# A planned graph-attention kernel: one shared set of five edge-weight places, new durations in its planner, and the last attention but one kept for the end

## The chip, the cores and the metric

The kernel runs on one core of one Trainium2 chip. The metric is device time in microseconds; the median of three runs before the change is 3646.97 us (3645.85 to 3647.93). The core has a matrix engine (PE, TensorE), a vector engine (DVE), a scalar engine (ACT), GpSimd (POOL) and a queue engine for transfers (SP, SyncE). Each runs its own list of instructions strictly in the order in which the program wrote it, and waits on semaphores where it needs another's result.

## The reference

The input is 32 graphs of 512 nodes, with 512 float32 features per node (`x`) and a sparse 0/1 adjacency (`adj`). Two residual layers follow one another.

```python
# layer 0
h = relu(layernorm(x))
s = leaky_relu((h @ w_src)[:, :, None] + (h @ w_dst)[:, None, :] + b, 0.2)
x = x + softmax(where(adj + eye == 0, -inf, s), axis=-1) @ h
# layer 1: two graph attention layers over mask = adj > 0 or diagonal
h = relu(layernorm(x))
def gat(h, W, a_src, a_dst):            # per head
    xl = h @ W
    e = leaky_relu((xl . a_src)[:, None] + (xl . a_dst)[None, :], 0.2)
    return softmax(where(mask, e, -1e9), axis=source).T @ xl
h = elu(concat(gat(h, W1, ...) for 4 heads of 256) + b1)
x = x + gat(h, W2, ...)                 # one head of 512
         + b2
```

Per graph there are thus six matrices of 512 x 512 edge weights: one in layer 0, four for the heads of W1, one for W2.

## The kernel before

**Stages.** Per graph b the stages are: `layer0_scores` (layer norm, dot products with the two attention vectors on DVE at L384, edge weights), `layer0_out` (attention, added to x), `layer1_in` (layer norm, 16 transposes on PE, x spilled to DRAM), `layer1_project` (products with W1, by Strassen's scheme with seven products in place of eight; the sums of the quarters are `combine`, L881 on DVE or L882 on POOL), `layer1_scores` and `layer1_head` for the four heads, `layer2_project` (products with W2 and its edge weights), and `layer2_out` (attention, added to x, stored). The main loop at the end of the kernel writes them down so that stages of neighbouring graphs stand side by side: `layer2_out(b - 1)` after `layer1_project(b)`, `layer0_out(b + 1)` after the heads of b, `layer0_scores(b + 2)` before `layer2_project(b)`. All matmuls of the attentions are on L684, all of the projections on L900, transposes on L506 and L605.

**Edge weights.** `edge_weights` makes one matrix E of four tiles of 128 x 512. The row of source terms is spread over the partitions (by PE transposes, or through DRAM by two DMAs); four L643 on DVE take the masked maximum; L649 and L651 (four numbers per partition) make from it the bound m of each row; m is spread by four transposes on PE (L506) or through DRAM; then per tile ACT computes the leaky ReLU (L665), DVE subtracts m (L668), POOL adds the mask (L671) and ACT takes the exponential (L674). PE then reads E as the stationary side of `aggregate` (L684), DVE takes a reciprocal (L696 or L970) and scales and adds (L702 or L973). The heads of W1 then go through elu: for three of the four (TURNED) on ACT (L987, L990), DVE (L994), and a transposing DMA between two ACT copies (L558, L574); for the last on ACT (L1009), DVE (L1013) and eight transposes on PE.

**What sets the order.** Nothing in the main loop runs at once. Each `op(...)` notes an operation with its engine or engines, its cost, what it reads and writes, and a head start or delay in rank. A cost is a pair: how long the engine is occupied, and when the result is there (for DMAs more). `Plan.run` then makes drafts: a list schedule in which each engine takes, whenever it is free, the ready operation of lowest rank, with 60 ns for a signal between engines; each first draft is ranked anew by the latest times that follow from it. The draft that ends first by the planner's own costs is written out as the program, so the costs decide the order on each engine, but not how long anything takes on the chip. Operations with `lock=True` on DVE and POOL are kept from overlapping each other in the draft; L649 and L651 have no lock, L1013, L671 and L882 have one.

**Places.** Each buffer of the plan belongs to a kind with a fixed number of places. A buffer takes a free place with its first operation and returns it after its last. Kinds named in the tuple of `Plan(slots, (...))` give their places out strictly in the order in which the program first names the buffers; other kinds give them to whichever operation is ready. Before, "E" has three places (heads, and the sums of the projections: one place for W1, two for W2) and "E_one" two (layer 0 and W2); both are given out in turn. All these places have the same shape, [128, 4, 512] float32.

**The end.** Graph 30's last attention (`layer2_out(B - 2)`) is split: `EARLY = 1` of its four tiles stands in the last round of the loop, before the heads of graph 31, and the other three after the last `layer2_project`, followed by the attention of graph 31.

The adjacency is loaded by `load_adj` (L725, on POOL's queue, with cast); the first load has a cost of its own. L758 adds the identity to it for layer 0, L761 turns it into a mask, and a transposing DMA makes the transposed mask.

Of the kernel before, what the change touches and what calls it, by code (L numbers as in the profile page):

```python
# [16 lines left out]
P = 128  # L17
# [229 lines left out]
def on_act(n, per_partition=0):  # L247

    one = n / 1.2 + (95.0, 140.0, 280.0)[per_partition]
    return one, one + 60.0  # L250

# [17 lines left out]
def kernel(  # L269
# [24 lines left out]
    nc = tc.nc  # L294
    B, N, D = x.shape
    H, F = att_src1.shape
    HF = H * F
    T = N // P
# [22 lines left out]
    def places(kind, n, shape, dtype=F32, pool=big):  # L321
# [12 lines left out]
        "xl2": places("xl2", 1, [P, T, 2 + D + 1]),  # L334
        "E": places("E", 3, [P, T, N]),
        "E_one": places("E_one", 2, [P, T, N]),
        "v": places("v", 4, [P, 2, F]),
# [114 lines left out]

    def scores_2(att):
        part = const.tile([P, KH, 2], F32, name="part")
        for k in range(KH):
            (q, r), kk = QUARTER[k // (KH // 2)], k % (KH // 2)
            lo, hi = w2_s[q][:, kk, :], w2_s[r][:, kk, :]
            for i in range(2):
                op(
                    "DVE", on_dve(W2),  # L460
                    lambda lo=lo, i=i, k=k: dot(lo[:, 2:], flat(att[1])[:, i * D : i * D + W2 - 2], part[:, k, i : i + 1]),
                    W["w2"]((q, kk)) + att[1](i), W["w2"](("part", k)), -LATER, lock=True,
                )
                op(
                    "DVE", on_dve(W2),
                    lambda lo=lo, hi=hi, i=i: dot(hi, flat(att[1])[:, i * D + W2 - 2 : (i + 1) * D], lo[:, i : i + 1]),
# [68 lines left out]
    def evict(src, dst, src_of, dst_of, n, bias=None, psum_half=False):  # L535
# [12 lines left out]

        op(("ACT", "DVE"), (on_act(n, bias is not None), on_dve(n)), (by_act, by_dve), src, dst)

    def turned(values_of, src, place, results_of, dst):
# [4 lines left out]
        op(  # L556
            "ACT", (1040.0, 1100.0),
            lambda: nc.scalar.copy(  # L558
# [19 lines left out]

        op("ACT", (1160.0, 1220.0), pair, src, dst)

# [52 lines left out]

    def edge_weights(kind, scores, ac, lines, k, mask_max, mask, near):

# [18 lines left out]

        E = Buffer(kind)
        m_row = (
# [61 lines left out]
    def load_adj(b, m):  # L718
# [67 lines left out]
    def layer0_scores(b):  # L786
        rstd, nmr = layernorm(X[b])
        h0, ac = Buffer("h"), Buffer("ac")
        for t in range(T):
            relu_normed(h0, X[b], t, rstd, nmr)  # L790
            for i, w in ((1, ws_r), (0, wd_r)):
                op(
                    "DVE", on_dve(D), lambda t=t, w=w, i=i: dot(h0.at[:, t, :D], w, ac.at[:, i, t : t + 1]),
                    h0(t) + W["w0"](0, 1), ac((i, t)), lock=True,
# [8 lines left out]

        L0[b] = (h0, edge_weights("E_one", scores, ac, in_lines(first(ac, 2), scores, 2) if b else None, 0, m0, m0T, not b))

# [143 lines left out]
    def layer1_scores(b, h):  # L949
# [8 lines left out]
        ac, lines = AC[b]  # L958
        return edge_weights("E", ac(0), ac, lines, 2 * j, m1T, m1, True)

# [71 lines left out]
    def layer2_project(b):  # L1032
# [19 lines left out]
        )  # L1052
        L2[b] = (edge_weights("E_one", ac(0), ac, in_lines(first(ac, 2), ac(0), 2) if b < B - 1 else None, 0, m1T, m1, b == B - 1), xl)

# [18 lines left out]

    EARLY = 1
    load_x(0)
# [63 lines left out]
```

## Time and profile before

| | |
|---|---|
| runs | 3647.93, 3645.85, 3646.97 us; median 3646.97 |
| the profiled execution | 3648.51 us, of it 3646.7 from the first to the last instruction (the span) |
| granted clock of PE, mean | 0.994 |
| busy, share of the span | PE 97%, its weight loads 83%, DVE 78%, ACT 62%, POOL 39% |
| moved by DMA | 378.82 MB, 104 GB/s |

The profile is of one execution. "L684" is line 684 of the kernel; a line can be that of a helper that many stages call, so the names of the tiles (E, E_one, h, xl, pair) tell the stage. In a row of the timeline the columns are start and duration in us, engine, line, instruction, result and operands, a count, and in brackets how long the engine was idle before and what ended that. In the view of waits: who waited for whom, us in total, how often, the longest. A group's row has the busy time in us, the mean of one in ns, then the engine's idle time before it and what ended it. Each matmul of this kernel stands in the records twice (the four heads make 2048 matmuls in the code and 4096 records on L684), so 16 records are 8 matmuls. The times of matmuls include their pipelined ends; their issue is closer together.

### The profile page before, as it was taken

To read this page: it belongs to the slowest core of one execution; us is meant where nothing else is said; L and a number is where in the kernel's file an instruction comes from. 1 tells how busy PE (TensorE), PEld (TensorE's weight loads), DVE (VectorE), ACT (ScalarE), POOL (GpSimd) and SP (SyncE) were. 2 spreads that over 40 slices of the span, in tenths; PEclk is the share of its full clock that TensorE was granted. 3 is DMA by queue.
4 is the path that set the end of the run, shared out by engine and by line. 5 is a ranking of instruction groups with operands and counts; after the bars stand their busy time and mean duration, and the time that the engine had idled before them with its cause. 6 is when DMAs were issued, how large, how long until landed. Compare 5 with 4: busy or idle time off the path is not lost.

```text
span 3646.7 us, 50543 instructions
## 1 busy us (share of the span) xinstructions
PE 3542.6 (97%) x16852; PEld 3036.1 (83%) x16852; DVE 2851.2 (78%) x7367; ACT 2264.6 (62%) x3929; POOL 1424.6 (39%) x1279
## 2 busy tenths in 40 slices
PE   4899999999999999999999999999999999999998
PEld 3788888888888888888888888888888888888887
DVE  7978778877778877778787788877787877887755
ACT  2666566665666665666666667655666656666554
POOL 4534334434334343334343344343343433343422
PEclk9999999999999999999999999999999999999999
DMA  6244433444433444334443334443334443344321
GB/s 172 77 105 119 104 92 104 100 121 113 96 96 103 104 121 112 90 96 105 115 116 98 95 103 99 125 116 86 97 110 105 119 108 89 103 103 118 105 73 41
DMA packets 510374, 378.82 MB, mean 104 GB/s; under 512 B 348344, under 2 KB 386976, under 8 KB 510112
## 3 DMA queue, kind: packets, MB, share of 16 engines
q1 hardware_dynamic: 476320, 342.03, 32.8%
q0 software_dynamic: 33792, 33.56, 6.1%
q8 instruction: 132, 2.16, 0.2%
q14 instruction: 130, 1.06, 0.1%
HBM read 257.16 MB, written 68.01 MB: 89 GB/s over the span
## 4 chain that ended last, share of the span: by engine, by line
PE 80%; DVE 14%; ACT 2%; issue 1%; DMA 1%; POOL 0%; DVEq 0%; ACTq 0%; SPq 0%
PE acc L684 45%; PE acc L900 32%; DVE junk L384 5%; PE acc L506 3%; DVE v L1013 1%; DVE hT L881 1%; DVE hT L545 1%; DVE col L521 1%; DVE col L649 1%; ACT h L529 1%; DVE v L973 1%; PE acc L605 1%; DVE junk L643 1%; DVE E L881 1%; DVE xl L913 1%
## 5 line engine op out<-in xcount | busy, mean ns | idle before, releaser
L684 PE MATMUL acc<-pair,E 128*128 128x257 f32 x4096 | 920.4, 379 | 2.4 <-ACT row L987 2.4
L684 PEld LDWEIGHTS acc<-pair,E 128*128 128x128 f32 x4096 | 771.7, 189 | 115.5 <-ACT row L987 2.8
L671 POOL TENSOR_TENSOR E<-E,m 128x512 f32<-128x512 f32 x512 | 605.1, 1211 | 455.3 <-DVE E L668 396.7
L900 PE MATMUL acc<-w_T,E 128*128 128x257 f32 (+1 forms) x2048 | 517.9, 380 | 0.8 <-POOL w_T L488 0.8
L684 PE MATMUL acc<-h,E_one 128*128 128x256 f32 (+1 forms) x2048 | 491.2, 381 | 8.6 <-ACT E_one L674 7.5
L684 PE MATMUL acc<-xl,E_one 128*128 128x257 f32 x1984 | 447.9, 381 | 2.7 <-ACT E_one L674 2.7
L643 DVE CUSTOM_DVE_ANT_0 junk<-m1T,acc 128x512 bf16<-128x512 bf16 x640 | 436.6, 682 | 11.4 <-PE acc L506 3.4
L900 PEld LDWEIGHTS acc<-w_T,E 128*128 128x128 f32 x2048 | 385.4, 189 | 61.0 <-POOL w_T L488 1.5
L684 PEld LDWEIGHTS acc<-h,E_one 128*128 128x128 f32 x2048 | 380.8, 191 | 63.6 <-ACT E_one L674 8.3
L684 PEld LDWEIGHTS acc<-xl,E_one 128*128 128x128 f32 x1984 | 371.8, 190 | 54.7 <-ACT E_one L674 3.1
L674 ACT ACTIVATE E<-E 128x512 f32<-128x512 f32 x512 | 315.6, 623 | 161.7 <-POOL E L671 161.4
L913 DVE TENSOR_TENSOR pair<-acc,pair 128x258 f32<-128x258 f32 (+1 forms) x390 | 165.4, 426 | 293.7 <-PE acc L900 219.2
L539 ACT COPY pair<-acc 128x258 f32<-128x258 f32 (+1 forms) x456 | 165.8, 370 | 320.5 <-PE acc L900 315.8
L665 ACT ACTIVATE E<-row,ac 128x512 f32<-128x512 f32 x512 | 341.1, 707 | 2.4 <-DMA row<-lines 2.4
L668 DVE TENSOR_TENSOR E<-E,acc 128x512 f32<-128x512 f32 x512 | 330.4, 678 | 6.5 <-PE acc L506 3.1
L671 POOL TENSOR_TENSOR E_one<-E_one,m0T 128x512 f32<-128x512 f32 x128 | 144.4, 1152 | 355.6 <-DVE E_one L668 355.6
L725 POOL DMA_DIRECT2D m<-in_adj_dram x64 | 51.5, 805 | 590.8 <-DVE col L643 540.7
L900 PE MATMUL acc<-w,hT 128*128 128x258 f32 x1024 | 265.5, 384 | 0.6 <-issue 0.5
L900 PE MATMUL acc<-w,E 128*128 128x257 f32 (+1 forms) x1024 | 264.2, 380 | 0.0
L702 DVE SCALAR_TENSOR_TENSOR x<-acc,r,x 128x256 f32<-128x256 f32 x512 | 239.7, 479 | 30.9 <-PE acc L684 22.8
L529 ACT ACTIVATE h<-x,col,col 128x512 f32<-128x512 f32 x256 | 187.6, 804 | 109.0 <-DVE col L521 109.0
L539 ACT COPY xl<-acc 128x257 f32<-128x257 f32 x218 | 77.6, 369 | 284.9 <-PE acc L900 284.8
(113 smaller groups left out, 6171.9 us busy)
## 6 DMA issues: line engine op xcount, KB each, us to landing
row<-lines SPq DMA_DIRECT2D x442, 256.0 KB, 3.4
x<-in_x_dram SPq DMA_DIRECT2D x32, 1024.0 KB
m<-in_adj_dram POOLq DMA_DIRECT2D x64, 512.0 KB, 6.3
spill<-x SPq DMA_DIRECT2D x32, 1024.0 KB, 4.2
x<-spill SPq DMA_DIRECT2D x32, 1024.0 KB
out_dram<-x SPq DMA_DIRECT2D x30, 1024.0 KB, 4.2
v<-row SPq DMA_TRANSPOSE x192, 2.7
out_dram<-x SPq DMA_DIRECT2D x8, 256.0 KB, 2.0
```

Source lines behind the costliest of these rows:

```text
L384: nc.vector.scalar_tensor_tensor(junk[:, : vector.shape[1]], values, 1.0, vector, op0=ALU.mult, op1=ALU.mult, accum_out=out)
L529: lambda: nc.scalar.activation(h.at[:, t, :D], X.at[:, t, :], AF.Relu, bias=nmr.at[:, t : t + 1], scale=rstd.at[:, t : t + 1]),
L539: nc.scalar.copy(dst_of(), src_of())
L643: lambda t=t: nc.vector.tensor_tensor_reduce(by_blocks(junk), mask_row(mask_max, t), by_blocks(a_row.at), 1.0, LOWEST, ALU.add, ALU.max, a ...
L665: lambda t=t: nc.scalar.activation(E.at[:, t, :], c_row.at, AF.Prelu, bias=a_of(t), scale=1.0, alpha=SLOPE),
L668: op("DVE", on_dve(N), lambda t=t: nc.vector.tensor_sub(E.at[:, t, :], E.at[:, t, :], m_row.at), m_row(*ROW) + E(t), E(t))
L671: lambda t=t: nc.gpsimd.tensor_add(by_blocks(E.at[:, t, :]), by_blocks(E.at[:, t, :]), mask_row(mask, t)),
L674: op("ACT", on_act(N), lambda t=t: nc.scalar.activation(E.at[:, t, :], E.at[:, t, :], AF.Exp), E(t), E(t))
L684: lambda s=s: nc.tensor.matmul(acc.at[:, :n], E.at[:, s, node_block(t)], of(s), start=(s == 0), stop=(s == T - 1)),
L702: lambda acc=acc, r=r, f=f, t=t: nc.vector.scalar_tensor_tensor(X.at[:, t, f], acc.at[:, :HD], r.at, X.at[:, t, f], op0=ALU.mult, op1=ALU. ...
L900: lambda k=k: nc.tensor.matmul(acc.at[:, :width], at[a]()[:, k, node_block(r)], weight_of(w, k, c), start=(first and k == 0), stop=(k == n ...
L913: op("DVE", on_dve(width), lambda: nc.vector.tensor_add(place(), acc.at[:, :width], place()), acc(0) + token, token)
```

## The change

The change alters no instruction and no size. It has four parts.

- "E" and "E_one" become one kind "E" with five places. It is taken out of the tuple of kinds given out in turn, so any operation that is ready can take a free place. `edge_weights` loses its parameter `kind`.
- ACT's costs in the planner: operations with one per-partition operand get 46 ns more of occupation (186 for 140), every result is there 130 ns after that (60 before); copies out of PSUM get a formula of their own (`on_act_copied`); the two copies around the transposing DMA become 945 for 1040 and 1062 for 1160.
- DVE's costs: the dot products with attention vectors are told as if 125 elements longer (130 ns), the masked maxima L643 as N + 10 for N + 60 elements. The first adjacency load is told to land after 11000 ns, not 5500.
- `EARLY = 0`: all four tiles of graph 30's last attention stand after the last `layer2_project`.

```diff
 def on_act(n, per_partition=0):
 
-    one = n / 1.2 + (95.0, 140.0, 280.0)[per_partition]
-    return one, one + 60.0
+    one = n / 1.2 + (95.0, 186.0, 280.0)[per_partition]
+    return one, one + 130.0
+
+
+def on_act_copied(n):
+    one = n / 1.2 + 52.0
+    return one, one + 160.0
...
-        "E": places("E", 3, [P, T, N]),
-        "E_one": places("E_one", 2, [P, T, N]),
+        "E": places("E", 5, [P, T, N]),
...
-    plan = Plan(slots, ("x", "spill", "m0", "m0T", "m1", "m1T", "h", "hT", "pair", "xl2", "E", "E_one", "v"))
+    plan = Plan(slots, ("x", "spill", "m0", "m0T", "m1", "m1T", "h", "hT", "pair", "xl2", "v"))
...
-                        "DVE", on_dve(F),
+                        "DVE", on_dve(F + 125),
...
-                    "DVE", on_dve(W2),
+                    "DVE", on_dve(W2 + 125),
...
-        op(("ACT", "DVE"), (on_act(n, bias is not None), on_dve(n)), (by_act, by_dve), src, dst)
+        op(("ACT", "DVE"), (on_act_copied(n) if bias is None else on_act(n), on_dve(n)), (by_act, by_dve), src, dst)
...
-            "ACT", (1040.0, 1100.0),
+            "ACT", (945.0, 1100.0),
...
-        op("ACT", (1160.0, 1220.0), pair, src, dst)
+        op("ACT", (1062.0, 1220.0), pair, src, dst)
...
-    def edge_weights(kind, scores, ac, lines, k, mask_max, mask, near):
+    def edge_weights(scores, ac, lines, k, mask_max, mask, near):
...
-                "DVE", on_dve(N + 60),
+                "DVE", on_dve(N + 10),
...
-        E = Buffer(kind)
+        E = Buffer("E")
...
-            "POOL", (1100.0, 5500.0) if first else (2200.0, 16000.0 if early else 8000.0), lambda: nc.gpsimd.dma_start(m.at, node_tiles(adj, b)),
+            "POOL", (1100.0, 11000.0) if first else (2200.0, 16000.0 if early else 8000.0), lambda: nc.gpsimd.dma_start(m.at, node_tiles(adj, b)),
...
-                    "DVE", on_dve(D), lambda t=t, w=w, i=i: dot(h0.at[:, t, :D], w, ac.at[:, i, t : t + 1]),
+                    "DVE", on_dve(D + 125), lambda t=t, w=w, i=i: dot(h0.at[:, t, :D], w, ac.at[:, i, t : t + 1]),
...
-    EARLY = 1
+    EARLY = 0
```

The three calls of `edge_weights` drop their first argument, and the other line of `scores_2` changes as the one shown.

More of the change, by code (lines that the diff above doesn't have):

```diff
@@ L464, in scores_2 @@
                 op(
-                    "DVE", on_dve(W2),
+                    "DVE", on_dve(W2 + 125),
                     lambda lo=lo, hi=hi, i=i: dot(hi, flat(att[1])[:, i * D + W2 - 2 : (i + 1) * D], lo[:, i : i + 1]),
@@ L802, in layer0_scores @@
         scores = c + ac(*((0, t) for t in ROW))
-        L0[b] = (h0, edge_weights("E_one", scores, ac, in_lines(first(ac, 2), scores, 2) if b else None, 0, m0, m0T, not b))
+        L0[b] = (h0, edge_weights(scores, ac, in_lines(first(ac, 2), scores, 2) if b else None, 0, m0, m0T, not b))
     def layer0_out(b):
@@ L958, in layer1_scores @@
         ac, lines = AC[b]
-        return edge_weights("E", ac(0), ac, lines, 2 * j, m1T, m1, True)
+        return edge_weights(ac(0), ac, lines, 2 * j, m1T, m1, True)
     def layer1_head(b, h, E):
@@ L1052, in layer2_project @@
         )
-        L2[b] = (edge_weights("E_one", ac(0), ac, in_lines(first(ac, 2), ac(0), 2) if b < B - 1 else None, 0, m1T, m1, b == B - 1), xl)
+        L2[b] = (edge_weights(ac(0), ac, in_lines(first(ac, 2), ac(0), 2) if b < B - 1 else None, 0, m1T, m1, b == B - 1), xl)
     def xl2_of(buf):
```

## Prediction

> **What bounds the kernel now.** I read the page first: its busy shares, its 40 slices, its chain of the work that ended last. TensorE carries the span, and the slices fall below 9 tenths for PE only at the two ends.
>
> ```profile
> PE 3542.6 (97%) x16852; PEld 3036.1 (83%) x16852; DVE 2851.2 (78%) x7367; ACT 2264.6 (62%) x3929; POOL 1424.6 (39%) x1279
> ```
>
> Busy PE time has pipelined ends in it, so I took the work from issue intervals. In the chain, 40 matmul records last 8.68 us, 0.217 us each, and 4 transposes 0.44 us, 0.110 each. The page counts 1492 transposes (520+512+256+16 on L506, 188 on L605), so 15360 of PE's 16852 are matmul records: 15360 x 0.217 + 1492 x 0.110 = 3497 us. The span is 3646.7: **150 us are all that any order of the work can win.** Next I asked for busy time by stretches. The kernel repeats every 110.81 us (the same L684 runs of 98 records stand in the chain at 2798.34 and 2909.16), from 190.4 to 3403.9 us 29 times:
>
> ```profile
> 2739.01:2849.82 110.81, 109.87 (x527) 94.42 (x526) 87.88 (x226) 70.84 (x124) 43.30 (x39) 1.00 0.39 105
> ...
> 3620.00:3647.00 27.00, 17.82 (x68) 14.54 (x68) 8.97 (x24) 4.33 (x8) 4.49 (x4) 0.77 0.10 39
> ```
>
> The columns are length, then busy us and instructions of PE, PEld, DVE, ACT and POOL, then clock and DMA. One period holds 480 records and 46 transposes: 104.2 + 5.1 = 109.2 us, so 1.6 us are lost in each, 46 us in 29. The remaining 104 us lie in the start (some 80) and the end (some 23). No other engine is full in a period (DVE 79%), so the losses are places where PE, which runs its list strictly in order, reached an instruction too early. The view of waits, PE alone, names two of them, each 30 times:
>
> ```profile
> PE acc L506 <- DVE col L651: 23.8, 30, 4.4
> ...
> PE acc L506 <- DVE v L1013: 9.8, 30, 1.9
> ```
>
> The timeline of one period gives their sizes as delay of PE's next start: 0.75 us at the transposes of m (L651), 0.40 at those of the last head's v (L1013), and 0.29 at L605, which waits for the dot products and L798 (25.6 us in 30 waits for the weight load, the first 9.7). Together **1.44 of the 1.6 us**. Why m is late:
>
> ```profile
> 2786.38 1.06 DVE L649 TENSOR_TENSOR col<-ac,col 128x4 f32<-128x4 f32 x1
> ...
> 2788.58 0.65 PE L506 MATMUL acc<-ident,col 128*128 128x128 f32 x4 [0.58 <-DVE col L651]
> ```
>
> L649 adds four numbers per partition, 0.15 us elsewhere, and here takes 1.06, while GpSimd runs four mask additions (L671) from 2782.92 to 2787.43. That is a collision of two engines, no misjudged duration. At the start, two misjudged durations show:
>
> ```profile
> 8.51 0.17 DVE L513 BATCH_NORM_AGGREGATE mv<-st 128x2 f32<-128x6 f32 x1
> 14.18 0.29 DVE L758 TENSOR_TENSOR m<-m,ident 128x128 bf16<-128x128 bf16 x1 [5.51 <-DMA m<-in_adj_dram]
> 14.39 0.17 DVE L513 BATCH_NORM_AGGREGATE mv<-st 128x2 f32<-128x6 f32 x1
> ```
>
> VectorE idles 5.51 us for the first adjacency, and the last step of the first layer norm stands behind that wait although its input came at 6 us.
>
> ```profile
> 73.17 0.38 PE L605 MATMUL acc<-ident,ac 128*8 128x128 f32 x1 [9.30 <-DVE ac L798]
> ...
> 78.66 2.01 PE L900 MATMUL acc<-w_T,E 128*128 128x258 f32 x8 [0.79 <-POOL w_T L488]
> ```
>
> Here PE stands 9.3 us behind dot products. And the end:
>
> ```profile
> 3543.56 3.79 PE L684 MATMUL acc<-xl,E_one 128*128 128x257 f32 x8 [2.70 <-ACT E_one L674]
> ...
> 3618.20 1.09 PE L506 MATMUL acc<-ident,ac 128*128 128x128 f32 x8 [0.70 <-ACT ac L539]
> 3622.29 1.11 PE L506 MATMUL acc<-ident,col 128*128 128x128 f32 x4 [3.00 <-DVE col L651]
> 3626.15 16.71 PE L684 MATMUL acc<-pair,E_one 128*128 128x257 f32 x64 [2.74 <-ACT E_one L674]
> ```
>
> From 3617.52 to 3626.15 PE does 12 transposes (1.3 us) and idles 7.3: the last weights are being made and nothing is left to run.
>
> **The change part by part.** It adds and removes no instruction and no DMA; every effect goes through the order that the planner writes and the places it gives. The sum is made against the profiled execution, 3648.51 us (span 3646.7 plus 1.8), 1.54 above the median 3646.97.
>
> *Costs of the dot products (L384).* Told until now: 256/0.96+70 = 337 ns for 256 wide, 603 for 512. The timeline has dot after dot at 23.30 and 23.76 (0.46 us, 256 wide) and at 2732.70 and 2733.43 (0.73, 512 wide). Told now: 467 and 733, so right. In a period, eight dots ended 8 x 0.13 = 1.04 us later than planned; with that known, L605 is put later among ready matmuls: I take its 0.29 us as gone.
>
> *Costs of ScalarE.* L665 is told 613 ns and 743 to the result, before 567 and 627; L674 651 to the result, before 581; copies from PSUM of 258 values 267 and 427, before 310 and 370.
>
> ```profile
> L665 ACT ACTIVATE E<-row,ac 128x512 f32<-128x512 f32 x512 | 341.1, 707 | 2.4 <-DMA row<-lines 2.4
> ...
> L649 DVE TENSOR_TENSOR col<-ac,col 128x4 f32<-128x4 f32 x192 | 54.9, 286 | 0.1
> ```
>
> 707 lies between the old 627 and the new 743, nearer to the new. The last head's L1009 has the same formula (0.72 measured), so v is expected 0.12 us later and its transposes come later; but most of that wait is L1013 at 1.70 us instead of 0.69 beside a GpSimd addition (L882, 1.27). Bounds 0 and 0.40 us; I take half, 0.20, as both causes are in it.
>
> *Cost of L643.* It falls from 666 to 614 ns, yet four in a row start 0.72 us apart (3525.75, 3526.47, 3527.20, 3527.93). So m, which needs four, is now planned 0.21 us earlier, in the wrong direction, at six places of a period. Against this stands L651's wait of 0.75: the planner holds no lock for L649, so whether the new order meets L671 there is chance. L649's mean of 286 against a usual 153 is 0.133 x 192 = 25.5 us, about one collision a period. Bounds for m: all 0.75 gone, or 6 x 0.21 = 1.25 us added and another collision of 0.75. Nearest is the row as it is; I take 0.20 as won, by the later placing that the ScalarE results force. Steady sum: 0.29 + 0.20 + 0.20 = 0.69 us x 29 = **20 us**.
>
> A rule weighed here: the Trainium skill, "SBUF — State Buffer", section "Who interferes with whom", says that a VectorE instruction with two SBUF inputs and a GpSimd instruction that reads SBUF exclude each other, and that whichever comes second blocks for the other's whole instruction. The trace agrees (1.06 against 0.15), and the rule speaks against the change, since nothing in it gives L649 a lock; by it alone the 0.20 of m would be nought and the steady sum 14 us.
>
> *First adjacency load.* Its time to landing is told 11 instead of 5.5 us; VectorE got it 12.7 us after its issue at 1.51. The layer norm's last step then stands before L758, and the chain through L516, L529, the dots and m starts up to 5.5 us earlier. What is late next is the mask: it lands at 14.18 whatever the order, and its transposed form is needed at L643 (24.82 now). Bounds 0 and 5.5 (a loss is excluded, since only work that has its input passes L758); I take 5.0, as VectorE, 17 to 19 busy of each 20 us from 20 to 100, is the start's limit and gets this time back.
>
> *The wait of 9.3 us.* The 64 dots on weights now cost 64 x 0.13 = 8.3 us more in the plan, and L605 will not be put ahead of ready products. But w_T comes at 78.66 in any order that leaves the dots where they are. Bounds 0 and 9.3; I take 2.5, near the lower end, since VectorE stays full. Start: **7.5 us**.
>
> *Five places of one kind.* No wait of PE in a period names a place, so I value it at nothing. Gain: within the above. Loss: layer-0 weights may take a place early and hold it through a whole stage; if one head's weights start one mask addition late (L671, 1.21 us) in each period, 35 us. What hides it now is that L671's engine is idle 61% of a period.
>
> *EARLY = 0.* One of four tiles of the attention of graph 30 (16 records, 3.5 us) moves behind the last projection in the program's order. With them move one L696 (0.16), two L702 (0.48 each) and one store of 256 KB on SP; the four stores of graph 31 stand behind it either way, and the last 13.9 us of matmuls cover it. Bounds: 3.5 us won in the hole of 7.3, or 3.5 lost in the one that ends at 3552, where it is now the filler. The tiles there are the only ready work, so most will be taken there again: I take **2 us** won.
>
> Sum: 20 + 7.5 + 2 = 29.5; 3648.5 - 29.5 = 3619, less 1.5 for the median: **3618 us**.
>
> **Rivals.** *More (12%):* all three waits go, 1.44 x 29 = 42, the start gives 14.8, the end 7.3: 64 us, 3583. For it: each cause sits at one place of the period. Against: collisions are not priced. *Only moved (12%):* the waits of a period come back elsewhere, 1.6 us again, and the start wins 5 that the end or VectorE partly takes: 3644. *Slower (26%):* m is planned too early. Place: L506 transposes behind L643, L649 and L651. Price: 6 x 0.21 = 1.25 us plus one more collision, 0.75, less 0.49 won at the other two: 1.5 x 29 = 44, less 9.5 at the ends, 34: up to 3681; with half the price (22 - 9.5), 3659; I give it 3665. It decides from where more is added at m than 0.49 + 9.5/29 = 0.82 us a period. For it: L643's told cost leaves the 0.72 of the timeline. Against: other told costs come nearer, and PE has ready matmuls at most places. *Not done:* the planner draws the same order; excluded, since dots 0.13 us longer change it.
>
> **How the numbers follow.** Forecast 50%; its own range is 3602 (steady 0.29 + 0.40 + 0.40 = 1.09 us, start 10, end 3.5) to 3636 (steady 0.29 alone, start 2.5, end nothing). Faster by over 0.2% (7.3 us, about what a measurement of this kernel can tell from no change), under 3639.7: the forecast and "more", 62%. Within: nearly all of "only moved", 11%. Slower, over 3654.3: 27%. The range leaves out some of "more" and the worst of "slower": 3588 to 3665.
>
> **What would show it.** Right: a period under 110.3 us; L605 without its wait; L758 no longer ahead of L513 near 14 us and the first attention before 30 us (33.59 now); PE's hole before the last 64 records under 6 us. L651's wait below 24 us speaks for my share, at 40 or more for the slower rival. Wrong: a period of 111 or longer, new waits of PE for E from L674, or a start that still reaches the second period at 190 us.

## The result and the profile after

The changed kernel takes **3625.17 us** (median of 4 runs, 3623.32 to 3626.74) against 3646.58 us before (4 runs, 3645.85 to 3647.93): a ratio of 0.9939, 95% interval 0.9927 to 0.9951, so 21.4 us or 0.6% faster. The profiled execution takes 3623.69 us, span 3621.9. The lines that matter stand four further down: L684 is now L688, L506 is L510, L649 is L653, L651 is L655, L900 is L904, L605 is L609, L665 is L669, L671 is L675, L674 is L678, L1013 is L1017.

The page first: PE's busy line and the shares of the chain that ended last.

```profile
PE 3537.2 (98%) x16852; PEld 3039.8 (84%) x16852; DVE 2814.5 (78%) x7468; ACT 2214.8 (61%) x3801; POOL 1500.5 (41%) x1306
...
PE 88%; DVE 2%; DMA 1%; issue 0%; POOL 0%; ACT 0%; DVEq 0%; SPq 0%; ACTq 0%
```

PE has the same 16852 records and nearly the same busy time; the span around them is shorter. The instructions are as many as before, but ACT has 128 fewer and DVE and GpSimd 101 and 27 more: some operations can run on either of two engines, and the plan chose anew. DVE's part of the chain is down to 2% (on the page of before it was 14%, with PE at 80%). To see where the time went, I cut both spans at the start of every 224th projection record (L900, L904 after; a graph has 224 of them): 32 marks, the first at 59.2 us before and 69.7 after.

| part of the span | before | after | difference |
|---|---|---|---|
| start to the second graph's mark | 188.4 | 194.1 | +5.7 |
| the 30 graphs from there to the last mark | 3325.4 | 3295.8 | -29.6 |
| the last mark to the end | 132.9 | 132.0 | -0.9 |

The sum is -24.8, the difference of the two spans. So the win is in the steady part, and the start lost. One period in the middle, and the end, by the view of windows (length, busy us of PE, PEld, DVE, ACT, POOL, then clock, DMA share and GB/s):

```profile
2721.91:2831.65 109.74, 109.70 (x527) 94.65 (x526) 86.28 (x228) 69.23 (x120) 46.61 (x40) 1.00 0.41 105
3600.00:3622.00 22.00, 16.99 (x64) 14.05 (x64) 5.34 (x14) 2.52 (x4) 3.67 (x4) 0.81 0.12 48
```

A period lasts 109.7 us instead of 110.81, with PE idle for 0.04 us in it instead of 0.94. The waits of PE:

```profile
PE acc L688 <- ACT E L678: 22.9, 6, 13.0
...
PE acc L510 <- DVE col L655: 15.6, 4, 11.1
PE acc L609 <- DVE ac L802: 7.6, 1, 7.6
```

The wait for m (L655) came 30 times before and comes 4 times now, and one of these four, 11.1 us at the start, is most of its total. The wait for v is no longer among the rows that repeat. As delay of PE's next start, two kinds of period now take turns: one loses 0.16 us at m and 0.26 at L609, the next (the one shown) 0.35 at m and nothing at L609. In the mean that is 0.25 and 0.13; before it was 0.75 at m, 0.40 at v and 0.29 at L605. And the 0.26 at L609 is not the old wait: ACT (L543) and L655 end it, not the dot products. The weight load, which waited for these 30 times before, does so twice, almost all of it at the start:

```profile
PEld acc L609 <- DVE ac L802: 8.4, 2, 8.0
```

**The start.** PE's timeline, beside that of before in the prediction:

```profile
13.00 0.45 PE L510 MATMUL acc<-ident,ac 128*128 128x128 f32 x1 [13.00 <-DVE junk L388]
...
29.96 1.11 PE L510 MATMUL acc<-ident,col 128*128 128x128 f32 x4 [11.11 <-DVE col L655]
44.10 17.12 PE L688 MATMUL acc<-h,E 128*128 128x257 f32 x64 [13.03 <-ACT E L678]
...
81.55 0.37 PE L609 MATMUL acc<-ident,ac 128*8 128x128 f32 x1 [7.61 <-DVE ac L802]
```

The first transposes run at 13.00 us (18.78 before): the layer norm's last step no longer stands behind the first adjacency. But the first attention (64 records) starts at 44.10 us, where it was 33.59. What held it is on the two engines that make its weights, DVE and GpSimd:

```profile
28.49 0.69 DVE L516 BATCH_NORM_STATS2 st<-x 128x6 f32<-128x512 f32 x1 [5.75 <-DMA x<-in_x_dram]
...
29.10 0.15 DVE L653 TENSOR_TENSOR col<-ac,col 128x4 f32<-128x4 f32 x1
...
29.77 0.14 DVE L655 SCALAR_TENSOR_TENSOR col<-col 128x4 f32<-128x4 f32 x1
```

```profile
39.70 2.40 POOL L492 TENSOR_TENSOR w_T<-w,w_T 128x1020 f32<-128x1020 f32 x1 [4.00 <-DMA w<-in_L_gnn_W_dram]
42.06 5.22 POOL L675 TENSOR_TENSOR E<-E,m0T 128x512 f32<-128x512 f32 x4
```

DVE waits 5.75 us for the *second* graph's x (L516) with the first graph's m (L653, L655) behind it in its list, and GpSimd waits 4.00 us for a weight matrix of W2 (L492) with the first graph's mask additions (L675) behind it. In the first 40 us the DMA engines are full in both kernels (a share of 0.98 and 1.09 in the windows 0 to 20 and 20 to 40 us after, 0.99 and 1.10 before), so whatever is loaded second comes late.

**The end** has not changed its shape. The last three starts on PE:

```profile
3593.10 1.09 PE L510 MATMUL acc<-ident,ac 128*128 128x128 f32 x8 [0.70 <-ACT ac L543]
3597.19 1.11 PE L510 MATMUL acc<-ident,col 128*128 128x128 f32 x4 [3.01 <-DVE col L655]
3601.05 16.99 PE L688 MATMUL acc<-pair,E 128*128 128x257 f32 x64 [2.74 <-ACT E L678]
```

From the eight transposes to the four of m there are 4.09 us and from there to the last weights 3.86, exactly as before. The tiles that `EARLY = 0` allows for this hole ran as filler at 3519.84 and later.

### The profile page after: what moved, and what is told of

Its sections match the earlier page's. It is cut to its first block, busy times and chain, and to the rows that moved or that the text cites. A ratio compares the mean times of both kernels' runs of the same rounds, so it can differ in the third digit from the quotient of the medians.

```text
span 3621.9 us, 50432 instructions
## 1 busy us (share of the span) xinstructions
PE 3537.2 (98%) x16852; PEld 3039.8 (84%) x16852; DVE 2814.5 (78%) x7468; ACT 2214.8 (61%) x3801; POOL 1500.5 (41%) x1306
## 4 chain that ended last, share of the span: by engine, by line
PE 88%; DVE 2%; DMA 1%; issue 0%; POOL 0%; ACT 0%; DVEq 0%; SPq 0%; ACTq 0%
PE acc L688 44%; PE acc L904 39%; PE acc L510 4%; DVE junk L647 1%; PE acc L609 1%; DVE E L672 0%; POOL E L675 0%; DMA lines<-row 0%; DMA row<-lines 0%; DVE x L706 0%; DVE v L977 0%; ACT acc L635 0%; ACT E L669 0%; DVE col L655 0%; DVE col L653 0%
## 5 line engine op out<-in xcount | busy, mean ns | idle before, releaser
L675 POOL TENSOR_TENSOR E<-E,m 128x512 f32<-128x512 f32 x640 | 759.4, 1215 | 545.8 <-DVE E L672 413.7
L688 PE MATMUL acc<-pair,E 128*128 128x257 f32 (+1 forms) x4160 | 935.0, 380 | 5.9 <-ACT E L678 3.9
L688 PEld LDWEIGHTS acc<-pair,E 128*128 128x128 f32 x4160 | 783.0, 189 | 122.0 <-ACT E L678 4.7
L678 ACT ACTIVATE E<-E 128x512 f32<-128x512 f32 x768 | 472.9, 623 | 218.1 <-POOL E L675 217.1
L904 PE MATMUL acc<-w_T,E 128*128 128x257 f32 (+1 forms) x2048 | 515.7, 380 | 0.2 <-POOL w_T L492 0.2
L669 ACT ACTIVATE E<-row,ac 128x512 f32<-128x512 f32 x760 | 507.5, 710 | 3.2 <-DMA row<-lines 3.0
L672 DVE TENSOR_TENSOR E<-E,acc 128x512 f32<-128x512 f32 x768 | 491.7, 675 | 19.0 <-ACT acc L635 11.7
L688 PE MATMUL acc<-h,E 128*128 128x257 f32 (+1 forms) x2048 | 487.0, 382 | 16.3 <-ACT E L678 16.3
L688 PE MATMUL acc<-xl,E 128*128 128x257 f32 x1984 | 448.9, 380 | 2.7 <-ACT E L678 2.7
L688 PEld LDWEIGHTS acc<-h,E 128*128 128x128 f32 x2048 | 385.0, 191 | 70.8 <-ACT E L678 17.5
L904 PEld LDWEIGHTS acc<-w_T,E 128*128 128x128 f32 x2048 | 385.3, 190 | 56.3 <-POOL w_T L492 0.6
L688 PEld LDWEIGHTS acc<-xl,E 128*128 128x128 f32 x1984 | 371.2, 190 | 53.3 <-ACT E L678 2.9
L543 ACT COPY pair<-acc 128x258 f32<-128x258 f32 (+1 forms) x400 | 147.6, 370 | 297.3 <-PE acc L904 293.5
L675 POOL TENSOR_TENSOR E<-E,m0T 128x512 f32<-128x512 f32 x128 | 144.7, 1155 | 353.5 <-DVE E L672 353.5
L543 ACT COPY xl<-acc 128x257 f32<-128x257 f32 x190 | 68.8, 369 | 331.3 <-PE acc L904 331.3
L904 PE MATMUL acc<-w,hT 128*128 128x258 f32 x1024 | 269.6, 383 | 0.0
L904 PE MATMUL acc<-w,E 128*128 128x257 f32 (+1 forms) x1024 | 267.7, 381 | 0.0
L977 DVE SCALAR_TENSOR_TENSOR v<-acc,r,b_r 128x256 f32<-128x256 f32 x512 | 244.5, 478 | 9.2
```

The source lines that it names most:

```text
L543: nc.scalar.copy(dst_of(), src_of())
L669: lambda t=t: nc.scalar.activation(E.at[:, t, :], c_row.at, AF.Prelu, bias=a_of(t), scale=1.0, alpha=SLOPE),
L672: op("DVE", on_dve(N), lambda t=t: nc.vector.tensor_sub(E.at[:, t, :], E.at[:, t, :], m_row.at), m_row(*ROW) + E(t), E(t))
L675: lambda t=t: nc.gpsimd.tensor_add(by_blocks(E.at[:, t, :]), by_blocks(E.at[:, t, :]), mask_row(mask, t)),
L678: op("ACT", on_act(N), lambda t=t: nc.scalar.activation(E.at[:, t, :], E.at[:, t, :], AF.Exp), E(t), E(t))
L688: lambda s=s: nc.tensor.matmul(acc.at[:, :n], E.at[:, s, node_block(t)], of(s), start=(s == 0), stop=(s == T - 1)),
```

## Experiments

Four theories were open after the result: **costs** (the prediction's: the new durations move PE's waits away), **places** (five shared places do it, which the prediction valued at nothing), **end** (`EARLY = 0`), and **luck** (any redraw of the plan gives another period). Each run is compared with runs of the kernel before on the same chip, and its period is the time from graph to graph in the middle of its own trace.

**e1_costs: the new durations alone,** old places, `EARLY = 1`.

```diff
-    one = n / 1.2 + (95.0, 140.0, 280.0)[per_partition]
-    return one, one + 60.0
+    one = n / 1.2 + (95.0, 186.0, 280.0)[per_partition]
+    return one, one + 130.0
...
-                "DVE", on_dve(N + 60),
+                "DVE", on_dve(N + 10),
```

and the same for the dots, the copies and the adjacency, as in the change.

> The kernel before with all new durations of the planner, but the old places (three and two, in turn) and the old split of the last attention. Theory 'durations': the gain of the change is in the steady periods and comes from the planner's durations alone: period 109.7 to 110.1 us (before 110.82, changed kernel 109.72), total 3620 to 3630. Rival 'places': the shared places made the gain: period 110.6 or more, total 3643 to 3655. Rival 'redraw' (any new draw of the order moves the time by as much): no say on the sign, anything from 3615 to 3680.

Measured 3654.18 us against 3647.61: 1.0017 (1.0007 to 1.0026), slower. The first row of PE's waits:

```profile
PE acc L511 <- DVE col L656: 41.4, 32, 13.1
```

The wait for m is there 32 times, with 0.93 us of delay in a period (L656 is L651 of before), the period 110.75 us and the second mark at 190.8. In its periods the waits for v and for the dots at L605 are gone, 0.69 us together. Nearly all of that comes back elsewhere: 0.18 more at this m, 0.13 at a second one, 0.12 at the transposes of h behind ACT (L534), the rest in smaller delays. The costs do take away two of the three waits, as the prediction had it, and hardly any time. **Costs falls.**

**e2_pool: five shared places alone,** with the old durations.

```diff
-        "E": places("E", 3, [P, T, N]),
-        "E_one": places("E_one", 2, [P, T, N]),
+        "E": places("E", 5, [P, T, N]),
...
-    plan = Plan(slots, (..., "xl2", "E", "E_one", "v"))
+    plan = Plan(slots, (..., "xl2", "v"))
...
-        E = Buffer(kind)
+        E = Buffer("E")
```

> The kernel before with the five shared places alone, old durations. Theory 'durations': the three waits of a period stay (0.75, 0.40, 0.29 us), period 110.5 to 111.3, total 3640 to 3660. Rival 'places': period 109.7 to 110.0, total 3620 to 3630. Rival 'redraw': anything from 3615 to 3680.

Measured 3623.41 us against 3647.61: 0.9933 (0.9918 to 0.9948), the whole effect of the change. One period of it:

```profile
2720.94:2830.97 110.03, 109.87 (x528) 94.60 (x527) 87.99 (x228) 70.20 (x120) 45.52 (x40) 1.00 0.38 106
```

and its waits:

```profile
PE acc L604 <- DVE ac L797: 14.5, 18, 11.8
...
PE acc L505 <- DVE col L650: 9.7, 6, 4.9
```

0.31 us are lost at L604 (the wait for the dots, L605 before) and 0.24 at m; the v wait is gone. **Places stands.** By the three parts of the span (187.7, 3305.1, 130.0) it wins 20.3 us in the steady part and 2.9 at the end.

**e3_early: `EARLY = 0` alone.**

```diff
-    EARLY = 1
+    EARLY = 0
```

> The kernel before with the last attention but one kept wholly for the end, nothing else. Theory 'filler': its four tiles are the only ready work after the last first projection and run there whatever their place in the program, so the hole of 7.3 us before the last 64 records stays: total 3645 to 3648. Rival 'my prediction': the hole is filled in part, total 3644 to 3645 (2 us won).

Measured 3647.27 us: 1.0 (0.999 to 1.0009). Its end:

```profile
3615.50 1.09 PE L506 MATMUL acc<-ident,ac 128*128 128x128 f32 x8 [0.70 <-ACT ac L539]
```

From here to the last 64 records are 7.95 us, as before. The four tiles are taken in the earlier holes, from 3542.68 on, since there they are the only ready work. **End falls.**

**e4_tiny: one nanosecond more for L643,** a change without a meaning.

```diff
-                "DVE", on_dve(N + 60),
+                "DVE", on_dve(N + 61),
```

> The kernel before with one duration of the planner changed by 1 ns (masked maxima told one element longer), a change that means nothing: it measures what a new draw of the order alone does. Theory 'durations': the draw is nearly the same, total 3640 to 3654 (within 0.2%), period 110.6 to 111. Rival 'redraw': a change that means nothing moves the time by as much as the whole change did, 20 us or more either way.

Measured 3647.63 us: 1.0001 (0.9992 to 1.001), a period of 110.82 us and the same three waits. But in the planner's order on PE only 77 of 9172 operations stand elsewhere than before, so this is hardly a new draw, and **luck stays open** here. The other kernels say more: in e1_costs 6680 of them stand elsewhere, and the period is still 110.75 us.

What is it about the places? "E" and "E_one" were given out in turn, and apart from each other. Two runs part these.

**e5_free32: three places and two, as before, but not in turn.** An operation that opens two buffers of one kind must then find two free places, so the planner's test for a free place counts them.

```diff
-    plan = Plan(slots, (..., "xl2", "E", "E_one", "v"))
+    plan = Plan(slots, (..., "xl2", "v"))
...
-                first = min(vacant[buf.kind], default=None)
+                nth = sum(o.kind == buf.kind for o in new[: new.index(buf)])
+                first = sorted(vacant[buf.kind])[nth] if len(vacant[buf.kind]) > nth else None
```

> The kernel before with its three and two places as separate kinds, old durations, old split; only the rule that both kinds are given out strictly in turn is dropped (and the planner checks that an operation which needs two places at once finds two). Theory 'turn': what held the heads' weights back was the rule, not the number: period 109.9 to 110.3 us, total 3618 to 3630 as with the five shared places (3623.4). Rival 'number': the heads needed the two places of the other kind: period 110.6 or more, total 3640 to 3655.

Measured 3642.01 us against 3647.5: 0.9983 (0.9973 to 0.9992). Its period and its waits:

```profile
2735.90:2846.72 110.82, 109.87 (x527) 94.42 (x526) 87.90 (x226) 70.87 (x123) 43.30 (x39) 1.00 0.39 105
```

```profile
PE acc L507 <- DVE col L652: 24.3, 30, 4.8
...
PE acc L507 <- DVE v L1014: 7.5, 29, 0.7
```

The period is that of before to the hundredth, with its three waits; the 5 us come from the start (186.5) and the end (130.0), with 1.8 in the 30 graphs. Giving up the turn wins nothing in a period.

**e6_four: four shared places, free.**

```diff
-        "E": places("E", 5, [P, T, N]),
+        "E": places("E", 4, [P, T, N]),
```

(against e2_pool)

> The five shared places alone, cut to four (old durations, old split, one place of memory left unused). Theory 'turn': nothing is lost, total 3618 to 3630, period 109.9 to 110.3. Rival 'number': the gain of 24 us shrinks or goes: total 3635 to 3660.

Measured 3643.18 us: 0.9987 (0.9978 to 0.9996), period 110.84, the same three waits (0.77, 0.40, 0.29 us). With one place less it keeps the period of before, and its start (185.4) and end (130.0) are as good as those of e5. So sharing as such does nothing in a period either; **the fifth place that any matrix can have** is what counts. Before, the two places of "E_one" stood apart, so the heads never had more than three.

**e9_turn5: five shared places, strictly in turn** (one profile; e2_pool with "E" left in the tuple, and e5's count).

```diff
-    plan = Plan(slots, (..., "xl2", "v"))
+    plan = Plan(slots, (..., "xl2", "E", "v"))
```

> The kernel before with five shared places, but given out strictly in turn (old durations, old split; the planner checks that an operation which needs two places finds two). Theory 'fifth place, free': sharing alone is of no use, since a layer-0 matrix named early then blocks the heads named after it: the period grows by many us, total over 3900. Rival 'number alone': five places do it in any order, total 3618 to 3630.

Measured 4241.64 us, beside 3648.65 of before. The first row of PE's waits:

```profile
PE acc L605 <- DVE ac L798: 314.5, 31, 11.2
```

Before, PE stood at this place 9.3 us once and 0.3 in each period; here it is some 10 in each. In turn, the W2 attention's matrix and the next layer 0's must take their places where the program names them, and everything named later waits for that. One shared kind needs the freedom; the freedom without the fifth place does nothing. (PE's granted clock fell to 0.935 in the mean, so the time holds some of that as well as the waits.)

**e7_adj_old: the change with the first adjacency told to land at 5.5 us, as before.**

```diff
-            "POOL", (1100.0, 11000.0) if first else ...
+            "POOL", (1100.0, 5500.0) if first else ...
```

> The changed kernel with the first adjacency load told to land after 5.5 us again, all else as changed. Theory 'late loads': the 11 us let the second graph's layer norm be put before m on VectorE and stood it there behind its own load, which cost the start 6 us (second graph's first product at 194.1 us against 188.4 before): it comes back to 186 to 190, total 3616 to 3621. Rival 'other loads': the planner misjudges those loads with either number, start at 192 to 197, total 3622 to 3630.

Measured 3616.87 us against 3647.5: 0.9912 (0.9895 to 0.9929), **8.3 us faster than the change**: the first attention is at 32.47 us and the second mark at 183.0 for 194.1, 11.1 earlier, of which the 30 graphs give 5.8 back (3301.6 for 3295.8).

**e8_loads: the change with the first loads told slower,** 300/1.35 = 222 bytes per ns for the fetches of weights and the first two x, which the plan held to be faster than the windows show (254 to 299 GB/s with the adjacencies in it).

```diff
-            op("SP", by_dma(4 * P * n), ...
+            op("SP", by_dma(4 * P * n * 1.35), ...
...
-            "SP", by_dma(4 * N * D), ...
+            "SP", by_dma(4 * N * D * (1.35 if b < 2 else 1)), ...
```

> The changed kernel with the planner told that the weights, vectors and the first two graphs' features move at 222 bytes per ns in place of 300 (durations of the plan alone, no transfer changes). Theory 'late loads': the order then waits for nothing at 23 to 28 and 36 to 40 us, first attention before 37 us (44.1 in the changed kernel, 33.6 before), second graph's first product at 184 to 189, total 3615 to 3620. Rival 'VectorE is full anyway': the start stays at 192 to 196, total 3622 to 3628.

Measured 3611.83 us: 0.9901 (0.9886 to 0.9916), period unchanged (109.73), second mark 184.2. The start on PE:

```profile
28.75 1.12 PE L510 MATMUL acc<-ident,col 128*128 128x128 f32 x4 [5.75 <-DVE col L655]
32.61 16.49 PE L688 MATMUL acc<-h,E 128*128 128x257 f32 x64 [2.75 <-ACT E L678]
```

The first attention is back at 32.61 us. Only told durations differ, and they remove the two waits shown above: DVE and GpSimd take the first graph's work before the late loads.

**e11_loads_adj_old: e8 with the adjacency told 5.5 us again.**

```diff
-            "POOL", (1100.0, 11000.0) if first else ...
+            "POOL", (1100.0, 5500.0) if first else ...
```

> The kernel with the loads told at 222 bytes per ns (3611.8) and the first adjacency told at 5.5 us again. Theory 'late loads': with the other loads told right, the 11 us are of use, and without them VectorE stands behind the adjacency for 5 us again: second graph's first product 1 to 5 us later than with 11 (184.2), total 3613 to 3618. Rival 'the 11 us only harm': total 3605 to 3610.

Measured 3622.95 us against 3648.65: 0.9931 (0.9914 to 0.9947), longer than expected. The second mark is at 188.1, 3.9 us later than in e8, and the 30 graphs take 5.1 more (3299.9 for 3294.8). So the adjacency's true landing wins if the other loads are told rightly too: 3.9 us at the start and 11.1 in the whole time (3611.83 against 3622.95). If they are not, it costs 11.1 at the start (194.1 against 183.0) and 8.3 in the whole (3625.17 against 3616.87).

**e10_nodot: the change with the dots told short again** (337 and 603 ns).

```diff
-                        "DVE", on_dve(F + 125),
+                        "DVE", on_dve(F),
...
-                    "DVE", on_dve(W2 + 125),
+                    "DVE", on_dve(W2),
```

and `on_dve(D)` likewise.

> The changed kernel with the dot products told short again (337 and 603 ns), all else as changed. Theory (my prediction's step): the wait of PE at L605 for the dots, 0.29 us a period before and 0.15 in the changed kernel, is back: period 109.9 to 110.2 (109.72 in the changed kernel), 6 to 14 us more over 29 periods; the start moves by up to 8 us either way. Rival 'the other durations made it': period stays at 109.7 to 109.8.

Measured 3610.84 us against 3648.65: 0.9895 (0.988 to 0.991). One period:

```profile
2819.40:2929.10 109.70, 109.62 (x527) 94.27 (x526) 87.05 (x227) 69.14 (x120) 47.30 (x41) 1.00 0.39 105
```

The weight load waits for the dots in every graph again:

```profile
PEld acc L609 <- DVE ac L802: 15.7, 30, 1.3
```

That is a delay of 0.24 us in each period (the 0.15 that the expectation puts there in the changed kernel is the other wait at L609, by ACT and L655). Yet the period is no longer (109.67), since m's delays went. The start is 8.5 us shorter (185.6) though its first attention comes late (45.43 us), and the whole some 14 us shorter than the change. So telling the dots their true duration takes their wait away, as predicted, and wins no time.

**e12_loads_lock: e8 with L649 and L651 locked against GpSimd in the plan.**

```diff
-    op("DVE", on_dve(T), lambda: nc.vector.tensor_add(z.at, ac.at[:, k + 1, :], amax.at), scores + amax(*ROW), z(0))
+    op("DVE", on_dve(T), lambda: nc.vector.tensor_add(z.at, ac.at[:, k + 1, :], amax.at), scores + amax(*ROW), z(0), lock=True)
...
-            z(0), m(0),
+            z(0), m(0), lock=True,
```

> The kernel with the loads told at 222 bytes per ns (3611.8), and L649 and L651 kept from overlapping GpSimd's additions in the plan. Theory 'collision': their mean comes down from 222 to under 170 ns, and the rest of the wait at m (0.17 us a period) goes: period 109.5 to 109.7, total 3604 to 3611. Rival 'the lock costs order': the plan has less room, collisions go, but the period is 109.8 or more, total 3613 to 3640.

Measured **3609.69 us** against 3648.65: 0.9892 (0.9877 to 0.9906), the fastest of all, but its interval lies on those of e8 and e10. Its period is the shortest, 109.45:

```profile
2710.80:2820.30 109.50, 109.33 (x526) 94.11 (x525) 89.95 (x227) 69.57 (x120) 48.36 (x41) 1.00 0.41 106
```

Yet the mean of L653 is 236 ns, above the 222 of e8 and far from the 170 expected: the lock keeps the two apart in the plan, and on the chip they meet all the same. The wait at m is gone from its periods nonetheless, so a stretched record costs time only where PE stands close behind it.

**What a fifth place changes in a period.** PE's largest loss was m, and m was late because L649 stood beside GpSimd's mask additions. The full timelines show the same spot in three kernels (lines left out). Before:

```profile
2782.92 4.51 POOL L671 TENSOR_TENSOR E<-E,m 128x512 f32<-128x512 f32 x4 [5.57 <-DVE E L668]
...
2786.38 1.06 DVE L649 TENSOR_TENSOR col<-ac,col 128x4 f32<-128x4 f32 x1
```

e2_pool:

```profile
1775.80 4.51 POOL L670 TENSOR_TENSOR E<-E,m 128x512 f32<-128x512 f32 x4 [6.22 <-DVE E L667]
...
1777.90 0.20 DVE L648 TENSOR_TENSOR col<-ac,col 128x4 f32<-128x4 f32 x1
```

after:

```profile
1776.19 4.51 POOL L675 TENSOR_TENSOR E<-E,m 128x512 f32<-128x512 f32 x4 [5.17 <-DVE r L700]
...
1780.40 0.32 DVE L653 TENSOR_TENSOR col<-ac,col 128x4 f32<-128x4 f32 x1
```

Four additions in 4.51 us start 1.13 us apart. Before, the fourth starts at 2782.92 + 3 x 1.13 = 2786.31; L649 comes 0.07 us later and ends at 2787.44, with it. In e2_pool L648 comes 0.16 us before the second one ends, and after L653 0.30 us before the last one ends; both end with it. The two lie beside GpSimd in all three kernels; **the phase within a GpSimd instruction makes the price.** I matched every record of this line with GpSimd's records in all traces. In each kernel a stretched record (0.18 us or longer) ends when the GpSimd instruction ends, with a median difference of 0.02 us:

| kernel | five free shared places | L649 stretched, of 192 | longer than 0.9 us | median start within the GpSimd instruction, us | period, us |
|---|---|---|---|---|---|
| before | no | 29 | 28 | 0.11 | 110.82 |
| e1_costs | no | 33 | 30 | 0.26 | 110.75 |
| e3_early | no | 29 | 26 | 0.11 | 110.83 |
| e4_tiny | no | 29 | 27 | 0.11 | 110.82 |
| e5_free32 | no | 32 | 27 | 0.11 | 110.82 |
| e6_four | no | 32 | 27 | 0.09 | 110.84 |
| e9_turn5 | no (in turn) | 34 | 31 | 0.17 | 129.71 |
| e2_pool | yes | 59 | 1 | 0.88 | 110.03 |
| after | yes | 35 | 0 | 0.74 | 109.72 |
| e7_adj_old | yes | 36 | 2 | 0.71 | 109.73 |
| e8_loads | yes | 35 | 1 | 0.74 | 109.73 |
| e10_nodot | yes | 34 | 0 | 0.54 | 109.67 |
| e11_loads_adj_old | yes | 35 | 1 | 0.75 | 109.75 |
| e12_loads_lock | yes | 64 | 2 | 0.73 | 109.45 |

Between 1000 and 3000 us each of the 18 waits of PE at m (of 0.09 us or longer) in before follows a stretched L649, 0.75 us of delay for 0.92 of stretch. After the change 9 of 31 such waits do, and they are short; in e10_nodot one wait at m is left and in e12_loads_lock none.

v has the same cause: before, 28 of the 64 L1013 start 0.11 us into a GpSimd addition (L882) and last 1.71 us, alone 0.69; after, none starts within one, and none in e1_costs, so that v goes with the new durations alone too. It is one collision of each kind in every graph, repeated as long as the order repeats.

That the fifth place is in use is plain on ACT. Before, the fourth head's matrix is first written here, by the timeline of ACT:

```profile
2789.84 0.71 ACT L665 ACTIVATE E<-row,ac 128x512 f32<-128x512 f32 x1
```

into the first of the four tiles, 1.1 us before the last record that reads the first head's matrix in the same place ends (ends of matmuls are modelled), while the W2 attention's place, last read at 2782.8, stays empty until the next graph. In e2_pool it is written here:

```profile
2764.89 1.34 ACT L664 ACTIVATE E<-row,ac 128x512 f32<-128x512 f32 x2 [0.84 <-PE acc L683]
```

into the place that the W2 attention has just left: ACT waited 0.84 us for PE's last record on its first tile. Counted from the first record of layer 0's attention in the same graph, the head starts 26.4 us later before the change, 20.0 in most graphs of e2_pool and 22.9 or 24.2 in most after.

**What the plan itself says.** The planner's own times can be worked out from each kernel's code, and by them the fifth place wins nothing: the period is 109.62 us in before, e5_free32, e6_four, e2_pool and after alike, and the drafts of e6_four and e2_pool end within 0.2 us of each other (3583.3 and 3583.1), where the chip parts the two kernels by 20. What differs is where L649 stands beside GpSimd. In before, e5_free32 and e6_four it is planned, in 28 graphs, 1.05 us into an addition told at 1.11, so at its very end; on the chip it comes some 0.1 us into the next addition, where it waits longest. In e2_pool nearly all that meet GpSimd are planned 0.9 to 1.1 us into an instruction and start there on the chip too; after the change they are planned at 0.5 or 0.9, and start there or when GpSimd is done. So the places change the order, the order sets the phase, and no cost of the planner holds the price of a phase. That five free places got a cheap phase is therefore luck as far as the planner goes; it held in all seven kernels that have them and in none of the seven others, though several orders within each group are nearly alike. A sixth place wasn't tried, nor the old places with L649 alone moved.

## Why the prediction was right, and where not

The number, 3618 us, lies 7 us under the time, well within its range, and "faster by over 0.2%" came. Its working was wrong in most terms, which partly cancel.

- **Five places of one kind: "No wait of PE in a period names a place, so I value it at nothing."** This is the step that failed. Alone they give 0.9933, the whole effect. The observation was true, and by the planner's own times so was the value: 109.62 us a period with four places and with five. What it left out is that other places give another order, and with it another phase against GpSimd, which the planner doesn't price: L649 longer than 0.9 us 28 times before and never after, 110.82 and 109.72 us a period. The prediction saw that chance at m, but did not tie it to the places. That the places were short could be read too: before, the fourth head's matrix takes its place as soon as the plan has it free, in nearly every graph, while the two places of "E_one" lie empty for 37 and 72 us in turn. The Trainium skill, "Perfetto Trace Analysis", section "Optimization Strategy", has the hint: a gap that repeats in the same way on the engine that should be saturated can mean too few buffers. Here the repeated gaps (0.75, 0.40 and 0.29 us, 30 times each) named DVE as releaser, and still four places or five decided between 110.84 and 110.03 us.
- **Steady part: 20 us predicted, 29.6 measured.** The mechanism, PE's three waits, was right and is where the time went: m from 0.75 to 0.25 (0.50 won, predicted 0.20), v from 0.40 to nothing (predicted 0.20), the dots' wait at L605 from 0.29 to nothing as predicted, with 0.13 of other waits new at L609. But the costs that were to win this time don't, as e1_costs shows: they remove v and the dots' wait and give the time back at m and elsewhere. With five places they add some 9 us more (e2_pool's 30 periods 3305.1 us, after 3295.8). That is about what e2_pool still loses to the dots (0.31 x 29 = 9.0), but e10_nodot has that wait and the same period, so which cost does it stays open. The start and the end give 8.4 back (187.7 + 130.0 against 194.1 + 132.0), so the whole change is no faster than the places alone.
- **L605.** That dots told rightly let PE come later to L605 is confirmed: the wait is there in every period of before, e2_pool and e10_nodot, which tell them short, and in no period of e1_costs and the change. That the delay would thereby be won is not: the time came back at other waits.
- **The collision at m.** "Whether the new order meets L671 there is chance" was right, and the price is finer than thought. The rule that I weighed, in the Trainium skill, "SBUF — State Buffer", section "Who interferes with whom", gives the shared ports to whoever issues first, for its whole instruction, and lets the other block. The trace agrees (both end at 2787.44), and I read it too coarsely: a late comer blocks only for what is left, 0.20 to 1.06 us for the same operation. A mean of all collisions is no price, since one phase repeats in each graph.
- **L643 in the wrong direction** ("slower", 26%). m did get later in e1_costs, from 0.75 to 0.93, and e1 is the slower kernel of the two; the rival had the right place and, with the old places, the right sign, at 0.2 us a period where it priced 1.5. Whether L643's cost did it was not parted from the other costs.
- **Start: 7.5 us won predicted, 5.7 lost.** The 5 us of the adjacency came at the first transposes (18.78 to 13.00) and were lost behind two loads that I had not looked at: x of the second graph and the last matrix of W2. "What is late next is the mask" was wrong; e8_loads shows that it was the told rate of the other loads. The wait at L605 fell from 9.30 to 7.61, 1.7 of the 2.5 that I took.
- **End: 2 won predicted, 0.9 measured,** less than single runs of one kernel differ by (3645.85 to 3647.93); alone `EARLY = 0` is worth nothing (e3_early), since the tiles are taken as filler earlier, as the prediction expected of most of them.
- Of the signs: the period under 110.3, L651's total under 24 us and L758 no longer ahead of L513 came; L605 came without its wait in the periods, though not at the start (7.61 us); the first attention before 30 us and a hole under 6 us at the end did not come, and the second mark lies at 194, which was to be a sign of being wrong.

## What to carry to other kernels

Where a program is written by a planner, a change of its places or costs leaves no wait that names it, only another order. Ask first what the planner's own times say of it. Here they gave the same period with four places and with five, so the 0.8 us a period that the chip won with the fifth place came from what the costs don't hold: where VectorE's operations meet GpSimd's. A collision that repeats once per round is worth what its phase leaves of the other instruction, times the rounds, as far as the bottleneck waits for it; so any change of the order can move the time. And one true duration among wrong ones may harm: the adjacency's cost 8 us with the other loads told wrong and won 11 with them told right, while the dots' took their wait away and left the kernel some 14 us slower.

## What was not expected of the hardware

- A VectorE addition of four numbers per partition lasts 0.15 us alone and 1.06 us where it starts 0.07 us into a GpSimd addition: it ends when the GpSimd instruction does (median difference 0.02 us in each of the traces).
- A plan's lock doesn't keep two engines apart on the chip: with it the stretched records of L653 are 64, where e8_loads has 35 (most of those added last under 0.22 us), though with the shortest period.
- In the first 40 us the DMA engines are full (0.98 to 1.10) at 241 to 299 GB/s, and a load of 1 MB issued beside others is there at 28.5 us; which engine it holds up changes with the order alone (e8_loads).
- PE's granted clock in the mean fell from 0.994 to 0.935 in e9_turn5, where PE was idle for 15.7 us in a period of 129.7.
